# A graph layer on one core: 84 and 88 single-row loads per block instead of 76 and 76, with seven counts per list

## The chip, the cores and the metric

The kernel runs on one core of one Trainium2 chip. The metric is the device time of one launch in microseconds (us), the median of three runs. Engines are named as in the profile: PE (TensorE, matmul), DVE (VectorE), ACT (ScalarE), POOL (GpSimd) and SP (SyncE). SP and ACT also issue ordinary DMAs from their instruction streams; POOL issues the indirect ones.

## The reference

A message-passing layer over 50,000 nodes of 128 features and 1,650,000 edges, sorted by destination. Each edge carries the source row through one of two matrices, chosen by its type; the messages are summed by destination, a self term and a ReLU follow, and the result is added to the input and normalised.

```python
# x (50000, 128) f32; src, dst, edge_type_2 (1650000,) int32, dst sorted
src, dst = (edge_index[0], edge_index[1])
Xs = X[src]
m_data = Xs @ W_data.T + b_data
m_ctrl = Xs @ W_control.T + b_control
msg = jnp.where((edge_types == 0)[:, None], m_data, m_ctrl)
agg = jax.ops.segment_sum(msg, dst, num_segments=X.shape[0])
out = agg + (X @ W_self.T + b_self)
return jax.nn.relu(out)
# outside: x = _layernorm(x + that, axis=-1)
```

## The kernel before, in words

**Blocks and steps.** The edge list is cut into `NBLK` blocks, here 430, each of two steps (`Q = 2`). In a step, most source rows are fetched by 14 (`R`) indirect gathers of 128 rows each, issued by POOL (L551): 28 gathers in a block. A list of `S = 76` further rows of the step is fetched one row at a time, each row of 512 bytes by a DMA of its own (`single_rows`, L568 to L593): the list of the first step by SP, that of the second by ACT. `F = 53` more edges per step are edges whose source the block's nodes provide, and are handled by DVE (`fill`). A block so covers `BE = 28 * 128 + 2 * (53 + 76) = 3842` edges. The first block and the last have gathers only; the last has what is left over, 17 gathers. Lists therefore exist for blocks 1 to 428.

**What a list issues.** The byte offsets of a list's rows lie in SBUF (`off_g`). `values_load_multi_w_load_instructions` (L580) loads up to `LOAD = 28` of them into the issuing engine's registers with one TENSOR_LOAD; then each row takes a register move and a DMA (L585). A list of 76 is so loaded in pieces of 28, 28 and 20. After every so many rows the engine raises the semaphore `issued[q]` by one (`mark`, L530): `R = 14` times in a list.

**What sets the order.** The schedule is written out by hand. In the turn of block `b`, the lists of block `b + FAR` (`FAR = 4`) are issued. Each list fills a buffer of its own, `y1` in the pool `one`; there are `ALONE = 10` of them, five per step, so a list's first row waits until PE has used the list five blocks earlier (matmul L613). On the other side, `pace` (L532) makes POOL wait before gather `k` of block `b`, from block 4 on, until step `k % 2`'s list of block `b + LAG` (`LAG = 1`) has been issued up to mark `k // Q`, that is `k // 2`. So POOL can't run further ahead than the lists of the next block.

**Other work on the same engines.** ACT, after every second list, computes the square root of the layernorm (`root`, ACTIVATE L677), and DVE's `store` (L683) waits for it. SP stores a block's output rows after its list (L691), loads a strip of `x` every eighth block (L490) and the edge tables every tenth (L196 to L200). DVE builds the one-hot matrices and their counts (L507, L515), and the filled-in indices (L395 to L416). PE multiplies one-hot by rows (L607) and by the single rows (L613).

Of the kernel before, what the change touches and what calls it, by code (L numbers as in the profile page):

```python
# [33 lines left out]
R = 14  # L34
W = 64
Q = 2
PASS = 7
B = 124
C = R * Q
F = 53  # L40
LATE = 10
FX = LATE + F
R1 = R + 1
# [2 lines left out]
SIZES = [P] * R  # L46
SIZE = sum(SIZES)
CE = Q * SIZE
S = 76
LOAD = 28  # L50
BE = CE + Q * (F + S)
NBLK = 2 + (E + LATE - CE) // BE
REST = E + LATE - CE - (NBLK - 2) * BE
REST_ROWS = [min(n, max(0, REST - q * SIZE - sum(SIZES[:r]))) for q in range(Q) for r, n in enumerate(SIZES)]
# [9 lines left out]
LAG = 1  # L64
# [18 lines left out]
TBL = GROUPS * GB  # L83
# [8 lines left out]
def plain(b):  # L92

    return b == 0 or b >= NBLK - 1
# [6 lines left out]
def straight(ctx, tc, c, x, x_t, edges_t, edges_f, edges_1, dst_first, first_p, out):  # L101
# [13 lines left out]
    nc = tc.nc  # L115
# [73 lines left out]
    def offsets(g):  # L189
        off = eds.tile([GB * Q, S], I32, name="off")  # L190
        nc.vector.tensor_scalar(off, one_g.pop(g), float(ROW), float((N - 1) * ROW), op0=ALU.mult, op1=ALU.min)
        off_g[g] = off

    def load_edges(g):
# [3 lines left out]
        nc.sync.dma_start(f.rearrange("b m f -> b (m f)"), edges_f[g * GB:(g + 1) * GB, :])  # L198
        one = eds.tile([GB * Q, S], I32, name="sd1", bufs=1)
        nc.sync.dma_start(one, edges_1[g * GB * Q:(g + 1) * GB * Q, :])  # L200
# [249 lines left out]
    def chunks_of(b, q):  # L450

        n = RCH if b == NBLK - 1 else C if b < NBLK else 0
        return range(q * R, max(q * R, min((q + 1) * R, n)))

    def column(k):
        return k // R * R1 + k % R

    def steps_of(b):
        return [q for q in range(Q) if len(chunks_of(b, q))]
# [12 lines left out]
    ys, ohs, cnts, accs, xTs, pos, hs, mvs, sds, os_ = {}, {}, {}, {}, {}, {}, {}, {}, {}, {}  # L472
# [54 lines left out]
    issued_no, asked, marks = [0] * Q, [0] * Q, {}  # L527

    def mark(q):
        (nc.scalar if q else nc.sync).sem_inc(issued[q], 1)  # L530
        issued_no[q] += 1

    def pace(b, k):

        if b < FAR:
            return
        q = k % Q
        if (b + LAG, q) in marks:
            n = marks[b + LAG, q] + k // Q
            if n > asked[q]:  # L540
                nc.gpsimd.wait_ge(issued[q], n)
                asked[q] = n

    def gathers(b, ks):
        i = pass_no[0] % SLOTS
        pass_no[0] += 1
        y = gat.tile([P, R, D], F32, name="y")
        for k in ks:
            pace(b, k)
            r = REST_ROWS[k] if b == NBLK - 1 else SIZES[k % R]  # L550
            copy = nc.gpsimd.indirect_dma_start(  # L551
                out=y[:r, k % R, :].bitcast(U8), out_offset=None, in_=x_rows,
                in_offset=bass.IndirectOffsetOnAxis(ap=idxs[b][:r, column(k):column(k) + 1], axis=0))
            copy.then_inc(landed[i], 16)
            tc.no_tile_sem_insts.add(copy.ins.name)
            tc.add_to_no_dep_group(f"rows{b}_{ks[0]}", copy.ins)
        seen[i] += 16 * len(ks)
        wait = nc.tensor.wait_ge(landed[i], seen[i])  # L558
        tc.declare_fence(wait.ins, group=f"rows{b}_{ks[0]}")
        return y  # L560
# [3 lines left out]
    got = [0] * ALONE  # L564
# [3 lines left out]
    def single_rows(b):  # L568
        if plain(b):
            return  # L570
        g, i = divmod(b, GB)
        for q in range(Q):
            j = alone_no[0] % ALONE
            alone_no[0] += 1
            marks[b, q] = issued_no[q]
            y = one.tile([S, D], F32, name="y1")
            for s0 in range(0, S, LOAD):
                n = min(LOAD, S - s0)
                at = i * Q + q
                _, regs = nc.values_load_multi_w_load_instructions(  # L580
                    off_g[g][at:at + 1, s0:s0 + n], engines=[ACT if q else SP], min_val=0, max_val=(N - 1) * ROW,
                    skip_runtime_bounds_check_because=CLAMPED)
                for k, r in enumerate(regs):
                    r = nc.s_assert_within(r, 0, (N - 1) * ROW, skip_runtime_bounds_check_because=CLAMPED)
                    copy = (nc.scalar if q else nc.sync).dma_start(y[s0 + k:s0 + k + 1, :].bitcast(U8),  # L585
                                               x_bytes[bass.ds(r, ROW)].rearrange("(p e) -> p e", e=ROW))
                    copy.then_inc(alone[j], 16)
                    tc.no_tile_sem_insts.add(copy.ins.name)
                    tc.add_to_no_dep_group(f"single{b}_{q}", copy.ins)
                    while issued_no[q] - marks[b, q] < (s0 + k + 1) * R // S:  # L590
                        mark(q)
            got[j] += 16 * S
            singles[b, q] = y, alone[j], got[j]  # L593

    def products(b, q, ks):
        of_step = chunks_of(b, q)
        if b == NBLK - 1:
            ys[b, q] = gathers(b, ks)
        elif ks[0] == of_step[0]:
            ys[b, q] = gathers(b, of_step)  # L600
        y = ys[b, q]
        if ks[0] == 0:
            accs[b] = ps.tile([P, Q, 3, W], F32, name="acc")
        acc = accs[b][:, q]
        for k in ks:
            r = REST_ROWS[k] if b == NBLK - 1 else SIZES[k % R]
            nc.tensor.matmul(acc[:, :2, :].rearrange("p t w -> p (t w)"), y[:r, k % R, :], ohs[b][:r, column(k), :],  # L607
                             start=k == of_step[0], stop=k == of_step[-1] and plain(b))
        if ks[-1] == of_step[-1] and not plain(b):
            y, landed_1, n = singles.pop((b, q))  # L610
            wait = nc.tensor.wait_ge(landed_1, n)
            tc.declare_fence(wait.ins, group=f"single{b}_{q}")
            nc.tensor.matmul(acc[:, :2, :].rearrange("p t w -> p (t w)"), y, ohs[b][:S, q * R1 + R, :], start=False, stop=True)  # L613
        if ks[-1] == of_step[-1] and q == steps_of(b)[-1]:
            for t in range(2):
                nc.tensor.matmul(accs[b][:, :q + 1, 2, :], to_row[:, t, :], cnts[b][:, :q + 1, t * W:(t + 1) * W],  # L616
                                 start=t == 0, stop=t == 1)
# [107 lines left out]

    columns(0)
    single_rows(1)
    spread(1)
    fill(1)
# [13 lines left out]
    for b in range(2, FAR):  # L743
        single_rows(b)
    made, fresh = 2, [2]
    ready = []
    for b in range(NBLK):
# [23 lines left out]
        if b == NBLK - 1:  # L771
            layer(b - 1)
            moments(b - 1)
            root(pair(b - 1))
            own_part(b)
            store(pair(b - 1))
            for done in pair(b - 1):
                store_rows(done)
            for step, ks in passes_of(b):
                if ks:  # L780
                    products(b, step, ks)
            break
# [3 lines left out]
        if b + FAR < NBLK:  # L786
            single_rows(b + FAR)
        for q, (step, ks) in enumerate(passes_of(b)):
            if ks:
                products(b, step, ks)  # L790
# [28 lines left out]
    b = NBLK - 1  # L819
# [340 lines left out]
```

## Time and profile before

| what | value |
|---|---|
| median of 3 runs | 15066.82 us (15066.48 to 15069.68) |
| the profiled execution, its own time | 15065.38 us |
| its span, first to last instruction | 15063.7 us |
| granted TensorE clock, mean | 0.671 |
| HBM read, written | 870.39 MB, 27.30 MB |
| DMAs issued by SP and by ACT for single rows | 32528 each |
| indirect gathers by POOL | 12012 and 17 in the last block |

How to read it: the span is that of the one profiled execution, and durations below are from it; its own time is 1.7 us above its span, and the median 3.1 us above. The busy times count an engine's work, not the issue of DMAs, register moves or semaphores: SP has no busy time at all, and ACT almost none, though both issue rows most of the time. Their instruction streams show as SPq and ACTq in the timeline.

### The profile page before, as it was taken

The page shows a single profiled execution, that of the slowest core. Times are in us where ns is not written, and L with a number is a line of the kernel's source. Part 1 is how long each engine was busy: PE and PEld are TensorE (multiplying, and loading weights), DVE is VectorE, ACT ScalarE, POOL GpSimd, SP SyncE. Part 2 cuts the span into 40 slices and gives each one's busy share as a digit, 9 for nine tenths or more (in the row PEclk, how much of TensorE's full clock was granted, in tenths as well). Part 3 has the DMA queues.
Part 4 walks back from the last instruction along what each step waited for, and adds up shares of the span by engine and source line. Part 5 has one row for each costly group of instructions (what it writes and reads, how often), then busy time and mean ns, then how long its engine had stood idle before and what let it go on. Part 6 is the DMA issues. An engine that isn't in the chain of part 4 may idle for free. (4 is left out here: it accounts for less than half of the span.)

```text
span 15063.7 us, 244090 instructions
## 1 busy us (share of the span) xinstructions
PE 5857.4 (39%) x32862; PEld 5479.9 (36%) x32863; DVE 12073.6 (80%) x11957; ACT 67.2 (0%) x222; POOL 11376.7 (76%) x12039
## 2 busy tenths in 40 slices
PE   3433333333333333333333333333333333333333
PEld 3333333333333333333333333333333333333333
DVE  9878888877877788888888887878788888887875
ACT  0000000000000000000000000000000000000000
POOL 7777777777777777777777777777777777777777
PEclk7666666666666666666666666666666666666666
DMA  2222222222222222222222222222222222222222
GB/s 64 60 62 60 61 61 60 62 60 61 62 60 60 62 60 60 62 60 60 61 60 60 63 60 60 61 60 62 60 60 62 60 60 61 60 61 62 60 59 57
DMA packets 588595, 914.45 MB, mean 61 GB/s; under 512 B 262747, under 2 KB 381952, under 8 KB 586944
## 3 DMA queue, kind: packets, MB, share of 16 engines
q0 software_dynamic: 384928, 789.04, 20.8%
q1 hardware_dynamic: 136522, 92.72, 2.4%
q10 hardware_dynamic: 65494, 16.98, 0.6%
q14 instruction: 1384, 11.34, 0.2%
q8 instruction: 267, 4.37, 0.1%
HBM read 870.39 MB, written 27.30 MB: 60 GB/s over the span
## 5 line engine op out<-in xcount | busy, mean ns | idle before, releaser
L551 POOL DMA_INDIRECT y<-in_x,idx x12012 | 11359.3, 946 | 3667.3 <-issue 3075.1
L607 PE MATMUL acc<-oh,y 128*128 128x128 f32 x24058 | 4774.6, 384 | 8916.1 <-PEq L558 8871.1
L607 PEld LDWEIGHTS acc<-oh,y 128*128 128x128 f32 x24058 | 4571.4, 293 | 9247.8 <-issue 5053.0
L515 DVE TENSOR_REDUCE cnt<-oh 128x256 bf16<-128x3840 f32 x430 | 2834.7, 6592 | 14.7
L507 DVE TENSOR_TENSOR oh<-col,small 128x3840 f32<-128x3840 f32 x430 | 1781.5, 4143 | 0.0
L416 DVE TENSOR_REDUCE by<-new 128x126 bf16<-128x1890 f32 x428 | 1497.0, 3498 | 14.6
L621 DVE TENSOR_TENSOR sums<-acc,sums 128x192 f32 x860 | 307.3, 357 | 1341.1 <-PE acc L616 1292.9
L395 DVE COPY small<-cb 128x30 f32<-128x30 f32 x428 | 82.0, 192 | 1219.7 <-PE small L423 1219.7
L400 DVE TENSOR_TENSOR new<-m,small 128x1890 f32<-128x1890 f32 x428 | 909.0, 2124 | 14.7
L397 DVE TENSOR_TENSOR m<-rk,small 128x1890 f32<-128x1890 f32 x428 | 908.9, 2124 | 14.6
L404 DVE TENSOR_REDUCE v_new<-new 128x30 f32<-128x1890 f32 x428 | 907.9, 2121 | 14.7
L413 DVE TENSOR_TENSOR new<-m,small 128x1890 f32<-128x1890 f32 x428 | 905.8, 2116 | 0.0
L613 PE MATMUL acc<-oh,y 76*128 76x128 f32 x1712 | 334.0, 276 | 0.0
L651 PE MATMUL po<-wmsgT,sums 128*124 128x128 f32 x1720 | 304.5, 300 | 0.0
L613 PEld LDWEIGHTS acc<-oh,y 76*128 76x128 f32 x1712 | 265.6, 195 | 0.0
L641 PE MATMUL po<-own_w,xT 128*124 128x256 f32 x860 | 262.3, 386 | 0.8 <-DVE h L657 0.8
L637 DVE TENSOR_TENSOR sums<-pl,sums 128x372 f32<-128x372 f32 x428 | 233.2, 545 | 14.9
L651 PEld LDWEIGHTS po<-wmsgT,sums 128*124 128x124 f32 x1720 | 221.5, 188 | 53.0 <-issue 1.6
L448 DVE TENSOR_TENSOR pl<-pl,xT 128x248 f32<-128x248 f32 x428 | 181.7, 425 | 46.6 <-DVE xT L501 2.7
L649 PE MATMUL po<-bias,sums 3*124 3x128 f32 x860 | 208.3, 322 | 1.2 <-DVE sums L621 1.2
L649 PEld LDWEIGHTS po<-bias,sums 3*124 3x124 f32 x860 | 125.2, 183 | 149.3 <-issue 147.4
L501 DVE COPY xT<-xw 128x124 f32 x430 | 111.7, 260 | 77.4 <-issue 74.2
(147 smaller groups left out, 2915.1 us busy)
## 6 DMA issues: line engine op xcount, KB each, us to landing
y<-in_x SPq DMA_DIRECT2D x32528, 0.5 KB
y<-in_x ACTq DMA_DIRECT2D x32528, 0.5 KB
y<-in_x,idx POOLq DMA_INDIRECT x12012
xw<-in_x_t SPq DMA_DIRECT2D x54, 496.0 KB
out<-o SPq DMA_DIRECT2D x430, 62.0 KB
sdt<-in_edges_t SPq DMA_DIRECT2D x43, 450.0 KB
sdt_f<-in_edges_f SPq DMA_DIRECT2D x43, 14.8 KB
sd<-in_edges SPq DMA_DIRECT2D x43, 5.9 KB
```

The costliest lines, as they stand in the source:

```text
L397: nc.vector.tensor_tensor(m, rk_g[g][:, i, :, None].to_broadcast([P, C1, FX]), rank_no_ps[:, None, :].to_broadcast([P, C1, FX]), op=ALU.is ...
L400: nc.vector.tensor_tensor(new.rearrange("p (q r) f -> p q r f", r=R1), m.rearrange("p (q r) f -> p q r f", r=R1), vf.rearrange("p (q f) -> ...
L404: nc.vector.tensor_reduce(v, new, AX.X, ALU.add)
L413: nc.vector.tensor_tensor(old, m, cb[:, :, None].to_broadcast([P, C1, FX]), op=ALU.mult)
L416: nc.vector.tensor_reduce(by, old.rearrange("p (q r) f -> p q f r", r=R1), AX.X, ALU.add)
L507: nc.vector.tensor_tensor(oh, col_g[g][:, i, :, None].to_broadcast([P, C1, 2 * W]), num_ps[:, None, :].to_broadcast([P, C1, 2 * W]), op=AL ...
L515: nc.vector.tensor_reduce(cnt, ohs[b].rearrange("p (q r) w -> p q w r", r=R1), AX.X, ALU.add)
L551: copy = nc.gpsimd.indirect_dma_start(out=y[:r, k % R, :].bitcast(U8), out_offset=None, in_=x_rows, in_offset=bass.IndirectOffsetOnAxis(ap ...
L607: nc.tensor.matmul(acc[:, :2, :].rearrange("p t w -> p (t w)"), y[:r, k % R, :], ohs[b][:r, column(k), :], start=k == of_step[0], stop=k = ...
L613: nc.tensor.matmul(acc[:, :2, :].rearrange("p t w -> p (t w)"), y, ohs[b][:S, q * R1 + R, :], start=False, stop=True)
L649: nc.tensor.matmul(po, a[0:3, 2, :B], bias, start=False, stop=False)
L651: nc.tensor.matmul(po, a[:, t, :B], c["wmsgT"][:, t * D:(t + 1) * D], start=False, stop=t == 1)
```

## The change

The list of a block's first step (SP) grows from 76 rows to 84, loaded in three pieces of 28; that of the second step (ACT) from 76 to 88, loaded in pieces of 32, 32 and 24. Each list raises its semaphore 7 times instead of 14, and POOL's wait before gather `k` asks for mark `k * 7 // 28`. A block covers `3584 + 106 + 172 = 3862` edges, so the edges fit into 428 blocks instead of 430, with 10 gathers in the last. Buffers of the lists have 88 rows. The arrays on the host are laid out to match.

```diff
-S = 76
-LOAD = 28
-BE = CE + Q * (F + S)
+SINGLE = (84, 88)
+LOADS = (28, 32)
+S = max(SINGLE)
+MARKS = 7
+BE = CE + Q * F + sum(SINGLE)
...
-            n = marks[b + LAG, q] + k // Q
+            n = marks[b + LAG, q] + k * MARKS // C
...
-            for s0 in range(0, S, LOAD):
-                n = min(LOAD, S - s0)
+            for s0 in range(0, SINGLE[q], LOADS[q]):
+                n = min(LOADS[q], SINGLE[q] - s0)
...
-                    while issued_no[q] - marks[b, q] < (s0 + k + 1) * R // S:
+                    while issued_no[q] - marks[b, q] < (s0 + k + 1) * MARKS // SINGLE[q]:
                         mark(q)
-            got[j] += 16 * S
+            got[j] += 16 * SINGLE[q]
...
-            nc.tensor.matmul(acc[:, :2, :].rearrange("p t w -> p (t w)"), y, ohs[b][:S, q * R1 + R, :], start=False, stop=True)
+            nc.tensor.matmul(acc[:, :2, :].rearrange("p t w -> p (t w)"), y[:SINGLE[q], :], ohs[b][:SINGLE[q], q * R1 + R, :], start=False, stop=True)
```

In ACT's stream, one square root and the list behind it, before the change (`off` holds the offsets, `y_5307` is the list's buffer; a row "x27" stands for 27 DMAs of a row each; moves and marks are not shown):

```order
L677 ACTIVATE sd<-mv,eps 124x2 [waits DVE_49]
L580 TENSOR_LOAD off
L585 DMA y_5307<-in_x 1x512 [waits PE_sequencer_49,PE_49]
L585 DMA y_5307<-in_x 1x512 x27
L580 TENSOR_LOAD off
L585 DMA y_5307<-in_x 1x512 x28
L580 TENSOR_LOAD off
L585 DMA y_5307<-in_x 1x512 x20
```

The same place with the change:

```order
L679 ACTIVATE sd<-mv,eps 124x2 [waits DVE_49]
L582 TENSOR_LOAD off
L587 DMA y_5678<-in_x 1x512 [waits PE_sequencer_49,PE_49]
L587 DMA y_5678<-in_x 1x512 x31
L582 TENSOR_LOAD off
L587 DMA y_5678<-in_x 1x512 x32
L582 TENSOR_LOAD off
L587 DMA y_5678<-in_x 1x512 x24
```

Nothing changes its place; the three pieces grow from 28, 28 and 20 rows to 32, 32 and 24.

In POOL's stream, the first gathers of block 4, where the waits for the marks begin (`issued0` is SP's semaphore, `issued1` ACT's), before the change:

```order
L551 DMA y<-in_x,idx 128x512 [waits DVE_49,PE_sequencer_49,issued0,PE_49]
L551 DMA y<-in_x,idx 128x512 [waits issued1]
L551 DMA y<-in_x,idx 128x512 [waits issued0]
L551 DMA y<-in_x,idx 128x512 [waits issued1]
L551 DMA y<-in_x,idx 128x512 [waits issued0]
```

The same place with the change:

```order
L553 DMA y<-in_x,idx 128x512 [waits DVE_49,PE_sequencer_49,issued0,PE_49]
L553 DMA y<-in_x,idx 128x512 [waits issued1]
L553 DMA y<-in_x,idx 128x512 x2
L553 DMA y<-in_x,idx 128x512 [waits issued0]
L553 DMA y<-in_x,idx 128x512 [waits issued1]
```

Before, every gather waits for a mark, SP's and ACT's in turn; now two in four do, for marks that stand for 12 rows of SP or 12 to 13 of ACT instead of 5 to 6.

More of the change, by code (lines that the diff above doesn't have):

```diff
@@ L1122 @@
         rest = a[CE:].reshape(TBL - 1, BE)
-        steps = rest.reshape(TBL - 1, Q, SIZE + S + F)
+        step_at = [sum(SIZE + s + F for s in SINGLE[:q]) for q in range(Q)]
         cols = np.full((TBL, Q, R1, P), pad, np.int32)
@@ L1127 @@
             cols[0, :, r, :n] = a[:CE].reshape(Q, SIZE)[:, at:at + n]
-            cols[1:, :, r, :n] = steps[:, :, at:at + n]
+            for q in range(Q):
+                cols[1:, q, r, :n] = rest[:, step_at[q] + at:][:, :n]
             cols[NBLK - 1, :, r, :n] = rest[NBLK - 2, :CE].reshape(Q, SIZE)[:, at:at + n]
-        cols[1:NBLK - 1, :, R, :S] = steps[:NBLK - 2, :, SIZE:SIZE + S]
+        for q, n in enumerate(SINGLE):
+            cols[1:NBLK - 1, q, R, :n] = rest[:NBLK - 2, step_at[q] + SIZE:][:, :n]
         if k == "src":
@@ L1133 @@
         fills = np.full((TBL * Q, FX), pad, np.int32)
-        own = steps[:NBLK - 2, :, SIZE + S:].reshape((NBLK - 2) * Q, F)
+        own = np.stack([rest[:NBLK - 2, step_at[q] + SIZE + n:][:, :F] for q, n in enumerate(SINGLE)], 1).reshape(-1, F)
         fills[Q:(NBLK - 1) * Q, LATE:] = own
```

## The prediction

> **What bounds the kernel now.** I read the page's busy times first, then POOL's groups and timeline, then the streams of SP and ACT, which the busy times leave out.
>
> ```profile
> PE 5857.4 (39%) x32862; PEld 5479.9 (36%) x32863; DVE 12073.6 (80%) x11957; ACT 67.2 (0%) x222; POOL 11376.7 (76%) x12039
> L551 POOL DMA_INDIRECT y<-in_x,idx x12012 | 11359.3, 946 | 3667.3 <-issue 3075.1 <-ACTq L530 254.6 <-SPq L530 228.4
> L551 POOL DMA_INDIRECT y<-in_x,sdt x17 | 16.0, 939 | 5.2 <-issue 4.0 <-PE acc L607 0.6 <-PE po L651 0.3
> 3.19 1.13 POOL L551 DMA_INDIRECT y<-in_x,idx  x1 [1.07 <-DMA idx<-in_edges_t]
> ...
> 7007.59 0.94 POOL L551 DMA_INDIRECT y<-in_x,idx  x1 [0.30 <-issue]
> 7008.84 0.94 POOL L551 DMA_INDIRECT y<-in_x,idx  x1 [0.30 <-issue]
> 7010.08 0.95 POOL L551 DMA_INDIRECT y<-in_x,idx  x1 [0.30 <-ACTq L530]
> ...
> 15048.96 0.88 POOL L551 DMA_INDIRECT y<-in_x,sdt  x1 [0.30 <-issue]
> ```
>
> No engine is over 80% busy, but POOL never stops. A gather takes 946 ns and is followed by 0.30 us, whether the profile names "issue" or a mark of ACT (L530) as the releaser: a gap that is the same with and without a wait is the cost of the next instruction, no wait. From the first gather at 3.19 to the last at 15048.96 there are 12028 intervals, 15045.77 / 12028 = 1.251 us each. A block of 28 gathers is 35.03 us, and 12029 gathers are the whole time but 3.2 us ahead and 15063.7 - 15048.96 - 0.88 = 13.9 us behind. DVE (12073.6 / 430 = 28.1 us a block) and PE have room.
>
> SP and ACT must issue one list each in these 35.03 us. How much of it they need shows in ACT's timeline at two places (start, length, rows issued in a run). Early, after an even start, and late:
>
> ```profile
> 15.34 94.72 ACTq L585 DMA_DIRECT2D y<-in_x  x226
> ...
> 808.40 65.19 ACTq L585 DMA_DIRECT2D y<-in_x  x152
> 873.76 0.29 ACT L677 ACTIVATE sd<-mv,eps 124x2 f32<-124x2 f32 x1 [67.18 <-issue]
> 875.88 64.12 ACTq L585 DMA_DIRECT2D y<-in_x  x152
> ...
> 1276.91 64.41 ACTq L585 DMA_DIRECT2D y<-in_x  x152
> 1341.50 0.29 ACT L677 ACTIVATE sd<-mv,eps 124x2 f32<-124x2 f32 x1 [66.44 <-DVE idx L408]
> 1343.89 36.29 ACTq L585 DMA_DIRECT2D y<-in_x  x83
> ```
>
> ```profile
> 7052.58 29.66 ACTq L585 DMA_DIRECT2D y<-in_x  x76
> 7086.98 29.68 ACTq L585 DMA_DIRECT2D y<-in_x  x76
> 7116.83 0.30 ACT L677 ACTIVATE sd<-mv,eps 124x2 f32<-124x2 f32 x1 [69.81 <-DVE at L430]
> 7123.15 6.77 ACTq L585 DMA_DIRECT2D y<-in_x  x19
> ```
>
> Early, ACT works without a pause: between the end of a list at 808.40 + 65.19 = 873.59 and the next one's first row at 875.88 lie 2.29 us, square root and register load included. From 808.40 to 1343.89 it issues 16 lists, **33.47 us a list**. It is faster than POOL, gets ahead, and then runs into its buffers: late, 7082.24 to 7086.98 are 4.74 us, of which 4.74 - 2.29 = 2.45 is a wait, and a list without it would be 29.66 + 2.29 = **31.95 us**. So ACT has between 1.6 and 3.1 us of a block to spare. SP has as little, by its timeline and, in the last row, its waits (us in total, times, longest):
>
> ```profile
> 806.46 30.89 SPq L585 DMA_DIRECT2D y<-in_x  x76
> 837.59 0.28 SPq L691 DMA_DIRECT2D out<-o  x1
> 840.03 30.85 SPq L585 DMA_DIRECT2D y<-in_x  x76
> 871.11 0.28 SPq L691 DMA_DIRECT2D out<-o  x1
> 873.63 30.75 SPq L585 DMA_DIRECT2D y<-in_x  x76
> SPq L585 <- PE acc L613: 803.6, 340, 4.0
> ```
>
> At full rate a list with its output store takes 840.03 - 806.46 = 33.57 us; over the whole span it waits 803.6 us for buffers, 803.6 / 428 = 1.9 us a list.
>
> **The change part by part.** *POOL.* Two blocks of 28 gathers go, and 17 gathers in the last become 10: 56 + 7 = 63 gathers fewer, 63 x 1.251 = **78.8 us** off, if POOL stays the bound. The span would be 11966 x 1.251 + 3.2 + 13.9 = 14986.6 us. The cover of POOL's pace is that both lists of the next block are issued in time; POOL waits for their marks.
>
> *ACT.* The price of a row, of a mark and of a register comes from these rows: four rows without a mark, two with one between them, and the loads of 28 registers and of 20.
>
> ```profile
> 7080.73 1.18 ACTq L585 DMA_DIRECT2D y<-in_x  x4
> 7080.35 0.62 ACTq L585 DMA_DIRECT2D y<-in_x  x2
> L585 ACTq DMA_DIRECT2D y<-in_x x32528: 227/228/617, 15.3 to 14891.8; - x200
> L580 ACTq TENSOR_LOAD <-off x1: 1947/1947/1947, 7062.0 to 7062.0; - x1
> L580 ACTq TENSOR_LOAD <-off x1: 1548/1548/1548, 7073.8 to 7073.8; - x1
> ```
>
> An issue itself lasts 0.228 us (min, median and max of all issues in the third row), so a row comes every (1.18 - 0.228) / 3 = 0.317 us, and with a mark after 0.62 - 0.228 = 0.39, so a mark is 0.07. Eight registers more make a load 0.40 us longer, 0.05 each. A list gains 12 rows, 12 x 0.317 = 3.80 us, and 12 registers, 0.60, and loses 7 marks, 0.49: **+3.9 us**. There are still three loads and half a square root in a list, and no DMA of another kind is on ACT. At full rate a list would take 31.95 + 3.9 = 35.9 us by the late rows, and 33.47 + 3.9 = 37.4 by the early ones; with the early rows' wider spacing (33.47 against 31.95, or 5%) on the new rows as well, 37.6. All three are over 35.03, so ACT has no pause left, and the 78.8 us saved on POOL are not seen.
>
> *SP.* Eight rows more, 2.54 us, eight registers, 0.40, seven marks fewer, 0.49 less: +2.45, and 33.57 + 2.45 = 36.0 us. That is over POOL too, but under what I take for ACT, so it is hidden there. What SP issues beside its list (stores, strips, edge tables) stays as it was.
>
> *POOL's waits.* It now asks for a mark before two gathers in four. The last mark asked in a block is the sixth of the seven, ACT's row 76 of 88, close to the end of the list, as before (mark 13 of 14). Coarser marks bunch POOL's waits but don't change how many rows must be out at a block's end, so I price them at nothing in either direction: the gather's gap is 0.30 us beside a mark or not.
>
> *Behind ACT.* The square root for a pair of blocks stands behind the list, and DVE's `store` waits for it; a late list holds DVE. DVE needs 28.1 us of a block that will last 36 or more, and builds indices five blocks ahead, so it catches up inside the pair. PE's matmul over 84 or 88 rows instead of 76 adds no instruction.
>
> **How the time follows.** ACT's first row starts at 15.3 us and it then issues 426 lists (blocks 1 to 426) without a pause, p us each; POOL is released for the end of block 425 with the last of them, and then has 28 + 10 gathers without marks left, 38 x 1.251 = 47.5, and 13.9 us of tail. With the 2.3 us that don't follow the last list: span = 15.3 + 426 p - 2.3 + 47.5 + 13.9 = 426 p + 74.4. The ends of p are 35.9 and 37.6. The kernel will be nearer the early rows, where ACT has no pause and issues at once with SP almost always; but SP, at 36.0, will wait for buffers about a microsecond a list, as it does late, so I take **p = 36.9**. That gives a span of 15793.8; the median of the runs shown lies 3.1 us over the profiled span, so **15797 us**, 4.8% over 15066.82. The ends give 15371 and 16095.
>
> **The rivals.** *POOL stays the bound*, 14986.6 + 3.1 = 14990 us, 0.5% faster. Its place is ACT's list and its price the 12 rows; it holds if a longer list fits into 35.03 us. From the most favourable 31.95 us only 3.08 may be added, and with 0.60 - 0.49 for registers and marks the 12 rows would have to come at (3.08 - 0.11) / 12 = 0.248 us each. The issue alone lasts 0.228, and no row shows a spacing under 0.317. For it speaks only that the late waits are the longer part of the trace. The Trainium skill, DMA: Bandwidth & Descriptors, section Issuing engines are not separate DMA queues, says that issuing from several engines saves only the sequencer's time for starting a DMA, which is usually small against the DMA; by that rule the added rows would cost next to nothing, and the time would be this rival's. Here the trace disagrees: the 0.317 us are what fills ACT's stream.
>
> *ACT is over POOL, but only just.* If the list runs as late and registers cost nothing, p is 31.95 + 3.80 - 0.49 = 35.3 and the time 426 x 35.3 + 74.4 + 3.1 = 15115 us, 0.3% slower. That needs SP under 35.3 as well, which its early 33.57 + 2.45 speaks against.
>
> *One row at a time for both streams.* If the 0.228 us of an issue keep the other stream out, 172 rows need 39.2 us a block, 426 x 39.2 + 77.5 = 16777 us. Early, 152 rows would need 34.66 but took 33.47, so the issues overlap somewhat; against this rival also stands that rows are mostly evenly spaced. The Trainium skill, Perfetto Trace Analysis, section on DMA instructions by HWDGE, says that the generator of descriptors is locked for one sequencer while it is used, and that a wait for the lock is part of the profiled time. By it the sum would move towards this rival; the 33.47 us show that at most a part of the 0.228 can be locked.
>
> **Chances.** ACT bound with p from 35.9 to 37.6: 0.88. POOL stays the bound: 0.04. Just over: 0.04, of which 0.01 within 0.2%. One row at a time or a further loss: 0.04. The range 15450 to 16100 leaves out the lowest fifth of a microsecond of p, which SP's own 36.0 makes unlikely, and the rivals, some 0.15 in all. A measurement of this kernel can tell about 0.2% from no change. Faster 0.04, same 0.01, slower 0.95.
>
> **What would show it.** In the changed profile ACT's timeline should have runs of 88 rows with about 2.5 us between them and no longer pause, a list every 36 to 37.6 us from the first to the last; POOL should wait visibly longer than 0.30 us on ACT's marks (L532) in every block, its busy share falling to some 72%; SP should still wait on PE for its buffers, about a microsecond a list; DVE should wait for the square root before L685. If POOL's gaps stay at 0.30 us, the ACT term is wrong. If ACT's list is shorter than 35.9 us, the price of a row, a register or a pause is; if POOL waits mainly on SP, the order of the two lists is.

## The result, and the profile after

The changed kernel takes **16111.9 us** (median of four runs, 16111.58 to 16114.0) against 15066.65 us before, 1.0694 times as long (95% interval 1.0676 to 1.0713). The profiled execution has a span of 16110.1 us.

The page of the changed kernel: busy times, and the groups of POOL's gathers and of DVE's wait for the square root (busy time and mean, then the idle time ahead of them and who ended it).

```profile
PE 6097.5 (38%) x32698; PEld 5539.4 (34%) x32699; DVE 12027.6 (75%) x11909; ACT 66.7 (0%) x221; POOL 11313.9 (70%) x11976
L553 POOL DMA_INDIRECT y<-in_x,idx x11956 | 11302.7, 945 | 4777.0 <-issue 3227.2
L685 DVE RECIPROCAL rstd<-sd 124x2 f32<-124x2 f32 x215 | 35.6, 166 | 3674.9 <-ACT sd L679 3674.9
```

Its waits (in total, times, longest), POOL's and then SP's:

```profile
POOL y L553 <- ACTq L532: 1421.6, 1127, 2.9
POOL y L553 <- SPq L532: 53.1, 170, 1.5
...
SPq L587 <- PE acc L615: 423.8, 165, 3.6
SPq L587 <- PEq L613: 140.3, 49, 5.0
```

A gather takes 945 ns as before, and there are fewer of them, but POOL now waits for ACT's marks: 1421.6 us in 1127 waits, of which 0.30 us each is the old gap, so some 1080 us are real. They are nearly all of the 1123 us by which the span, 16110.1 us, exceeds the 14986.6 us that POOL would have needed alone. They are not long, 2.9 us at most; POOL's timeline shows one:

```profile
7047.97 0.95 POOL L553 DMA_INDIRECT y<-in_x,idx  x1 [0.30 <-issue]
7050.95 0.94 POOL L553 DMA_INDIRECT y<-in_x,idx  x1 [2.03 <-ACTq L532]
7052.20 0.95 POOL L553 DMA_INDIRECT y<-in_x,idx  x1 [0.31 <-PE acc L609]
```

ACT's own timeline has no pause any more, early or late, and ends with the last list:

```profile
843.61 74.10 ACTq L587 DMA_DIRECT2D y<-in_x  x176
917.89 0.29 ACT L679 ACTIVATE sd<-mv,eps 124x2 f32<-124x2 f32 x1 [76.33 <-issue]
920.23 73.32 ACTq L587 DMA_DIRECT2D y<-in_x  x176
...
1073.96 24.29 ACTq L587 DMA_DIRECT2D y<-in_x  x64
...
7034.52 72.86 ACTq L587 DMA_DIRECT2D y<-in_x  x176
7107.57 0.29 ACT L679 ACTIVATE sd<-mv,eps 124x2 f32<-124x2 f32 x1 [75.09 <-issue]
7109.95 70.03 ACTq L587 DMA_DIRECT2D y<-in_x  x168
...
15977.03 69.64 ACTq L587 DMA_DIRECT2D y<-in_x  x176
```

From 843.61 to 1073.96 it issues six lists, 38.4 us each; from 7034.52 to 7109.95 two, 37.7 each. In between lies the point where SP, which needs less, runs into its buffers and begins to wait (564 us in all, 1.3 a list). Over the whole run a list takes (16110.1 - 74.4) / 426 = **37.64 us**, by the prediction's sum. That is where the time came from: a block is no longer as long as 28 gathers but as long as ACT's list.

One more thing changed. The windows view (mean share of the DMA engines' time that is busy, and GB/s, at the end of a row) from 4000 to 8000 us, before and after:

```profile
4000.00:8000.00 4000.00, 1559.38 (x8748) 1461.80 (x8748) 3205.76 (x3171) 16.84 (x57) 3023.74 (x3200) 0.67 0.23 61
```

```profile
4000.00:8000.00 4000.00, 1532.35 (x8133) 1391.87 (x8133) 2986.36 (x2935) 15.64 (x53) 2816.05 (x2980) 0.63 0.27 57
```

The DMA engines are busier (0.27 against 0.23) while they move less. The kernel before shows the same where both streams run without a pause: from 800 to 1344 us its share is 0.28, at the same 61 GB/s as later. So there were two questions: is it ACT's list that sets the pace, and why is the list 37.64 us and not the 36.9 of the forecast.

### The profile page after: what moved, and what is told of

Read it like the earlier page. It is cut to its first block, busy times and chain, and to the rows that moved or that the text cites. A ratio compares the mean times of both kernels' runs of the same rounds, so it can differ in the third digit from the quotient of the medians.

```text
span 16110.1 us, 253999 instructions
## 1 busy us (share of the span) xinstructions
PE 6097.5 (38%) x32698; PEld 5539.4 (34%) x32699; DVE 12027.6 (75%) x11909; ACT 66.7 (0%) x221; POOL 11313.9 (70%) x11976
## 5 line engine op out<-in xcount | busy, mean ns | idle before, releaser
L609 PEld LDWEIGHTS acc<-oh,y 128*128 128x128 f32 x23932 | 4466.1, 289 | 10137.5 <-issue 8047.2
L685 DVE RECIPROCAL rstd<-sd 124x2 f32<-124x2 f32 x215 | 35.6, 166 | 3674.9 <-ACT sd L679 3674.9
L425 PE MATMUL small<-ones_b,by 128*126 128x1 bf16 x426 | 73.0, 172 | 2696.2 <-DVE oh L509 2696.2
L388 PE MATMUL small<-v_f,row_of 74*128 74x126 bf16 x426 | 104.8, 247 | 2393.1 <-DVE at L432 2366.0
L615 PE MATMUL acc<-oh,y 84*128 84x128 f32 (+1 forms) x1704 | 396.4, 321 | 0.0
L643 PE MATMUL po<-own_w,xT 128*124 128x256 f32 x856 | 350.6, 502 | 0.8 <-DVE h L659 0.8
L653 PE MATMUL po<-wmsgT,sums 128*124 128x128 f32 x1712 | 345.4, 331 | 0.0
L615 PEld LDWEIGHTS acc<-oh,y 84*128 84x128 f32 (+1 forms) x1704 | 329.0, 240 | 0.0
L653 PEld LDWEIGHTS po<-wmsgT,sums 128*124 128x124 f32 x1712 | 253.9, 213 | 62.3 <-issue 22.7
```

Source lines behind the costliest of these rows:

```text
L653: nc.tensor.matmul(po, a[:, t, :B], c["wmsgT"][:, t * D:(t + 1) * D], start=False, stop=t == 1)
```

## The experiments

Theory A is the prediction's: each stream needs the sum of its own instructions, and the longer one sets the pace. Theory B is that the streams of SP and ACT share something behind them, so that the rows of both together count. The kernels are the changed one with other numbers; the short names are those of the runs.

**Each stream alone, and fewer rows beside ACT's 88.**

```diff
-SINGLE = (84, 88)
+SINGLE = (84, 76)    # a1, LOADS (28, 28)
+SINGLE = (76, 88)    # a2
+SINGLE = (28, 88)    # a3
```

> Lists of 84 rows (SP) and 76 (ACT), 7 marks each, 429 blocks. Theory (a stream that needs more than POOL's 35.03 us for its list sets the pace, whichever of the two): SP at full rate took 36.6 us a list of 84 in the changed kernel's early part, so about 36.3 here, 427 x 36.3 + 77 = 15580 us, POOL waiting on SP's marks, ACT pausing 2 us or more a list. Rival (only ACT's longer list costs, SP's fits): POOL stays the bound with 12004 gathers, 12004 x 1.251 + 20 = 15037 us.

> Lists of 76 rows (SP) and 88 (ACT), 7 marks each, 429 blocks. Theory (ACT's list alone sets the pace, and its rows come slower the more SP issues beside them): 37.0 to 37.4 us a list, 427 x 37.2 + 77 = 15960 us, SP pausing about 4 us a list. Rival (SP's issues don't touch ACT's): 37.6 us a list as in the changed kernel, 427 x 37.6 + 77 = 16130 us.

> SP's list cut to 28 rows, ACT's left at 88, 434 blocks. Theory (what the list takes over the sum of its parts, 37.6 against 35.9, is lost to SP issuing at the same time): ACT's list falls to 35.8 to 36.2 us, 432 x 36.0 + 77 = 15630 us, and nearly all rows stand 0.318 us apart. Rival (the rows are slowed by something else, POOL's gathers or the fetching of instructions): 37.4 us or more, 432 x 37.5 + 77 = 16280 us.

a1 took 15232.93 us, 1.0106 (1.0077 to 1.0136) of the 15075 us before. In its timeline SP has no pause, and a list takes 34.8 to 35.1 us:

```profile
7011.53 31.95 SPq L587 DMA_DIRECT2D y<-in_x  x84
7043.70 0.28 SPq L693 DMA_DIRECT2D out<-o  x1
7046.36 32.31 SPq L587 DMA_DIRECT2D y<-in_x  x84
7078.89 0.28 SPq L693 DMA_DIRECT2D out<-o  x1
7081.47 32.46 SPq L587 DMA_DIRECT2D y<-in_x  x84
```

With strips and edge tables it is (15230.8 - 74.4) / 427 = 35.5 us on average. So SP's part of the change costs time by itself, against the rival; but less than the theory's 36.3, which was read where ACT's list of 88 stood beside it.

a3 took 15792.66 us. ACT's list is (15791.0 - 74.4) / 432 = 36.4 us:

```profile
7067.78 69.89 ACTq L587 DMA_DIRECT2D y<-in_x  x176
7137.84 0.30 ACT L679 ACTIVATE sd<-mv,eps 124x2 f32<-124x2 f32 x1 [72.11 <-issue]
7140.29 59.80 ACTq L587 DMA_DIRECT2D y<-in_x  x150
```

The stream of ACT is the same as in the changed kernel, and SP issues 28 rows beside it instead of 84: 1.2 of the 37.64 us go. That is just over the theory's 35.8 to 36.2 and far from the rival's 37.4. I take the rest of ACT's list, 36.4, as its own; it is still 0.5 over the lowest sum of the forecast.

a2's launch took 36.8 ms, since with these lists the kernel's test of its own assumptions (the branch behind `found`) sent it through the general path after the blocks; only the first part of its trace is used. There ACT's list with 76 rows on SP is (7113.06 - 7040.09) / 2 = 36.5 us, hardly more than with 28 (ACT's timeline, and behind the dots SP's):

```profile
7040.09 70.45 ACTq L587 DMA_DIRECT2D y<-in_x  x176
7110.72 0.29 ACT L679 ACTIVATE sd<-mv,eps 124x2 f32<-124x2 f32 x1 [72.69 <-issue]
7113.06 70.03 ACTq L587 DMA_DIRECT2D y<-in_x  x176
...
7038.64 0.28 SPq L693 DMA_DIRECT2D out<-o  x1
7047.80 28.95 SPq L587 DMA_DIRECT2D y<-in_x  x76
7076.99 0.28 SPq L693 DMA_DIRECT2D out<-o  x1
```

The theory's 37.0 to 37.4 fails here: the loss doesn't grow evenly with SP's rows. It comes when SP is nearly always issuing; here it pauses, 9.2 us between 7038.64 and 7047.80 in this list. The rival's 37.6 fails too.

**The marks.**

```diff
-MARKS = 7
+MARKS = 14                # a4, lists of 84 and 88
```

```diff
-SINGLE = (84, 88)
+SINGLE = (76, 76)         # b3, MARKS 7, LOADS (28, 28)
```

> The changed kernel with 14 marks a list instead of 7, so that POOL's waits are as fine as before. Theory (a mark costs ACT 0.07 us and coarse marks cost POOL nothing): 426 x 7 x 0.07 = 209 us more, 16320 us. Rival (waiting on coarse marks is what slows POOL): faster than the changed kernel's 16112 us.

> The kernel before with 7 marks a list instead of 14, the lists at 76 rows each: the part of the change that is only marks. All theories: POOL is the bound with 12029 gathers, 15067 us, no difference; ACT and SP pause 0.5 us longer a list. If POOL waited on the coarser marks, it would be slower by what its gaps on L532 are over 0.30 us.

a4 took 16128.85 us, 17 more than the changed kernel, where theory A asked for 209, and not less, as coarse marks would have it. b3 took 15067.71 us, 1.000 (0.9991 to 1.001): the marks alone change nothing. Its early stretch, where both streams run without a pause, is the more telling:

```profile
805.59 64.00 ACTq L587 DMA_DIRECT2D y<-in_x  x152
...
1341.64 18.20 ACTq L587 DMA_DIRECT2D y<-in_x  x44
```

16 lists in 536.05 us are 33.50 us each, with 7 marks; before, with 14 marks, the same stretch had 33.47. At full rate a mark of ACT's stream costs nothing, as if the stream had slack. The lengths of the single issues in the traces show where the slack is: over these 16 lists ACT's issues last 0.263 us on average with 7 marks and 0.256 with 14. By 76 rows that is 0.5 us, as much as 7 marks of 0.07.

**As many rows in all, spread evenly.**

```diff
-SINGLE = (84, 88)
+SINGLE = (80, 80)         # b1, LOADS (28, 28)
+SINGLE = (78, 78)         # b2, LOADS (28, 28)
+SINGLE = (79, 79)         # b4, LOADS (28, 28)
```

> Lists of 80 and 80 rows, 7 marks each, 429 blocks: as many rows in a block as with 84 and 76, but neither stream near 35.03 us by its own sum (SP 35.3 - 4 x 0.375 = 33.8, ACT 36.4 - 8 x 0.375 = 33.4). Theory A (each stream's own list is the bound): POOL stays the bound, 12004 gathers, 12004 x 1.251 + 20 = 15037 us. Theory B (something that both streams share, such as the DMA engines behind them, takes so many rows of both in a time: 172 rows in 37.6 us, 160 in 35.4): 35.4 us a block again, 427 x 35.4 + 77 = 15190 us or a little more, both streams without a pause.

> Lists of 78 and 78 rows, 7 marks each, 430 blocks, 12015 gathers. Theory A: POOL is the bound, 12015 x 1.251 + 20 = 15051 us, 0.1% faster than before. Theory B: 156 rows in 156 / 160 x 35.4 = 34.5 us, under POOL's 35.03, so the same 15051 us.

b1 took 15148.4 us (15115.7 to 15159.62), 1.0056 (1.0041 to 1.0072) of before: theory A's 15037 fails, theory B's 15190 is near. Neither stream pauses, and ACT's 80 rows take 35.2 us:

```profile
7045.31 67.90 ACTq L587 DMA_DIRECT2D y<-in_x  x160
7113.39 0.29 ACT L679 ACTIVATE sd<-mv,eps 124x2 f32<-124x2 f32 x1 [69.89 <-issue]
7115.78 4.24 ACTq L587 DMA_DIRECT2D y<-in_x  x11
```

Where both streams run at full rate, then, 152 rows take 33.47 us and 160 take 35.24, **0.220 us for each row of either stream**. The changed kernel's early rows are of the same kind; there SP issues 14 lists between these two rows:

```profile
806.27 34.13 SPq L587 DMA_DIRECT2D y<-in_x  x84
...
1317.61 26.48 SPq L587 DMA_DIRECT2D y<-in_x  x64
```

That is 36.5 us a list of SP's beside 38.4 of ACT's, 84 / 36.5 + 88 / 38.4 = 4.59 rows in a microsecond, 0.218 us each. By 0.220 the 164 rows of a2 would need 36.1 us, less than the 36.4 that ACT's list takes in a3; so SP's 76 rows could add little there.

b2 took 15054.5 us, 0.9991 (0.9982 to 1.0000) of before, where both theories had 15051: POOL is the bound again, with 14 gathers fewer. The difference is at the edge of what can be told from no change.

> Lists of 79 and 79 rows, 7 marks each, 429 blocks, 12011 gathers: the longest even pair whose 158 rows x 0.220 us = 34.8 us stay under POOL's 35.03. Theory C: POOL stays the bound, 12011 x 1.251 + 20 = 15046 us, 0.15% faster than before and 0.06% faster than with 78 and 78. Theory A (each stream by its own sum) gives the same time but long pauses of both streams, 1 to 2 us a list; theory C a pause of 0.2 us.

b4 went through the general path like a2 (43.3 ms), and on a chip on which the kernel before took 19.48 ms instead of 15.07. Nothing is read from it.

**What the rows share: the gathers.** In c1 a gather has 64 rows, so that half of the gathered rows is missing from the sum; in e1 only 2 of 14 gathers of a step are issued, in f1 7 of 14.

```diff
-            r = REST_ROWS[k] if b == NBLK - 1 else SIZES[k % R]
+            r = min(64, REST_ROWS[k] if b == NBLK - 1 else SIZES[k % R])   # c1, gathers and matmuls
...
-        for k in ks:
+        for k in [k for k in ks if k % R < 2]:      # e1 (f1: < 7), gathers and matmuls
```

> The changed kernel (84 and 88 rows) with each gather cut to 64 rows of 128, and the matmuls over those 64 alone: half of the gathered rows is left out of the sum. Nothing in SP's and ACT's streams changes. Theory B with the DMA engines as what is shared: gathers take half their time there, so ACT falls to what it needs with SP nearly idle, 36.4 us a list, 426 x 36.4 + 77 = 15580 us. Rival (SP and ACT slow each other where they issue, whatever the DMA engines do): 37.5 us a list, 16060 us or more.

c1 took 15957.45 us; ACT's list is (7176.04 - 7026.85) / 4 = 37.3 us (the last row is ACT's issues over the run: shortest, median and longest in ns):

```profile
7026.85 72.13 ACTq L587 DMA_DIRECT2D y<-in_x  x176
...
7101.51 72.01 ACTq L587 DMA_DIRECT2D y<-in_x  x176
...
7176.04 23.95 ACTq L587 DMA_DIRECT2D y<-in_x  x63
...
L587 ACTq DMA_DIRECT2D y<-in_x x37488: 234/235/675, 15.7 to 15891.6; - x200
```

Half of the gathered bytes bring back 0.3 of 1.2 us: by the time alone that is nearer the rival, which had SP and ACT slow each other alone. But the last row shows something that need not come from the gathers: not one of ACT's issues is under 0.234 us, where in the changed kernel the shortest lasts 0.227 and the median 0.228. The two runs of e1 below, of one kernel, differ in the same way. 88 rows by 0.007 us are 0.6 us a list. Without them c1's list would be an estimated 36.7 us, and half-size gathers would bring back 0.9 of the 1.2. SP's issues don't have this (227 and 228 ns in both runs), and SP's lists between 800 and 1344 us go the same way: 36.5 us in the changed kernel, 35.6 in c1, 35.2 in e1. By this estimate c1 speaks against the rival too, and so does e1:

> The changed kernel (84 and 88 rows) with 2 of each step's 14 gathers and their matmuls; the other 12 are left out of the sum. SP's and ACT's streams are as they were, POOL has almost nothing to do. If the gathers take part in what slows the rows: ACT falls to what it needs with SP nearly idle, 36.4 us a list, about 15540 us. If SP and ACT slow each other alone: 37.2 us a list, as with half gathers, about 15880 us.

> Two of each step's 14 gathers, the others left out of the sum, beside the changed kernel on the same chip. If the gathers take part in what slows the rows: 36.4 us a list, 15578 us as in the call before. If SP and ACT slow each other alone: 37.2 us or more.

e1 took 15579.5 us on one chip and 15789.35 on another. The timeline of the second, where both streams are at full rate, ACT's rows and then SP's, and last ACT's issues in the first run and in the second:

```profile
1050.69 71.20 ACTq L590 DMA_DIRECT2D y<-in_x  x176
...
1198.23 1.76 ACTq L590 DMA_DIRECT2D y<-in_x  x5
...
1068.65 32.18 SPq L590 DMA_DIRECT2D y<-in_x  x84
1101.05 0.28 SPq L696 DMA_DIRECT2D out<-o  x1
1103.53 16.54 SPq L590 DMA_DIRECT2D y<-in_x  x43
...
L590 ACTq DMA_DIRECT2D y<-in_x x37488: 12/228/604, 15.5 to 15534.2; - x200
...
L590 ACTq DMA_DIRECT2D y<-in_x x37488: 3/235/588, 15.6 to 15743.8; - x200
```

SP's list takes 34.9 us and ACT's 147.54 / 4 = 36.9, both at once: 84 / 34.9 + 88 / 36.9 = 4.79 rows in a microsecond, where all gathers left 4.5 to 4.6. The 36.9 is the median issue of 0.235 us again; in the first run, at 0.228, ACT's list is (15577.8 - 74.4) / 426 = 36.4 us, as in a3, where SP had 28 rows. So with few gathers the two streams hardly slow each other, and with few rows on SP (a3) the gathers hardly slow ACT: it takes SP, ACT and the gathers together, as far as chips of two kinds can be set side by side.

These runs have a flaw. Both runs of e1, and those of d1, f0 and f1, were on chips on which the kernel before takes 19.46 to 19.48 ms (below, chips of the first kind are those with 15.07). The second e1, f1 and the last d1 stand beside f0, the changed kernel on the same chip, and are compared with it only; the first e1 has no such run beside it, and neither e1 nor f1 was run on a chip of the first kind.

> The changed kernel as it is, on the chip on which the three others of this call run: 16112 us and 37.6 us a list if the chip gives the kernel before its 15067 us, and the measure for the three others if not.

> The changed kernel with 7 of each step's 14 gathers, of 128 rows each, and their matmuls; the other 7 are left out of the sum. As many gathered bytes as with 14 gathers of 64 rows, half as many gathers. If what slows the rows goes by the number of gathers' DMAs: between the 37.2 us a list of half-size gathers and 36.4, about 36.6, 15670 us. If it goes by their rows or bytes: 37.2 us as there, about 15920 us.

> The changed kernel with 256 bytes of each single row, half of the single rows' features left out, beside the changed kernel on the same chip. Theory C (the shared cost goes by the number of rows): as the changed kernel, 37.5 us a list, 16100 us. Theory D (it goes by bytes): 36.4 us a list, 15580 us.

f0 took 21037.31 us, 1.08 times the 19456.57 of the kernel before on that chip: slower by about as much as on the other chips (1.07), but by SP's list, as POOL's waits in its trace show (us in total, times, longest):

```profile
POOL y L553 <- SPq L532: 4740.5, 1270, 6.5
POOL y L553 <- ACTq L532: 72.0, 137, 1.3
```

f1, with half of the gathers, took 15793.27 us, e1 15789.35. That the two agree is chance: in f1 POOL waits for SP (2190.0 us, against 40.3 for ACT), so SP's list sets the time, (15791.6 - 74.4) / 426 = 36.9 us, while in e1 it is ACT's. Against f0 SP's list falls from 49.2 to 36.9 us with half the gathers, so on these chips too the rows' slowness hangs on the gathers. f1's question, whether it goes by the number of gathers or by their bytes, was put for ACT's list and isn't answered. d1, single rows of 256 bytes instead of 512 (half of their features left out), took 20995.54, 21043.15 and 20920.46 us on three chips. The last stands beside f0's 21037.31, 0.6% less, but d1's own three times lie as far apart; so no share that goes by the rows' bytes is shown there, and on a chip of the first kind it was not measured.

**Where the 1.2 us sit.** The traces have the length of every issue. ACT's last 0.253 us on average in the changed kernel, 0.240 in a2 and 0.238 in a3. Between the changed kernel and a3 that is 88 x 0.0148 = 1.3 us a list, all of the loss: the rest of a list, 15.4 us, is the same in both, and the issues themselves stretch. The packets of ACT's rows stretch as well. By its counts queue q10 is ACT's, with two packets a row and 438 others in each run; before, changed kernel, a3 (packets, MB, share of 16 engines' span):

```profile
q10 hardware_dynamic: 65494, 16.98, 0.6%
...
q10 hardware_dynamic: 75414, 19.54, 1.4%
...
q10 hardware_dynamic: 76470, 19.81, 0.6%
```

By these shares a packet took about 22, 48 and 20 ns. Whether the slower packets hold up the issues, or only go with them, is not shown.

## Why the prediction was right, and where it wasn't

**Direction and the stream that sets the pace: right.** ACT lost its pause, POOL's 63 fewer gathers (11956 and 10 remain) are not seen, and the time is the number of lists by ACT's list. The sum's form holds within 2 us: ACT's 426 lists run from 15.7 to 15977.03 + 69.64 = 16046.67 us, which is 37.64 us each without using the sum, and 63.4 us come behind them where it had 47.5 + 13.9 = 61.4. ACT's next list begins 920.23 - 843.61 - 74.10 = 2.5 us after the last one, as forecast, POOL waits on ACT's marks (70% busy, 72 forecast), SP waits for PE 1.3 us a list (about one forecast), and DVE waits 3674.9 us for the square root and is hidden behind ACT.

**The size of p: wrong.** The step that failed is the one for ACT's list ("so I take **p = 36.9**"), a term of 36.9 us with ends at 35.9 and 37.6 that measured 37.64. 0.74 us by 426 lists are the 315 us between 15797 and 16112, and the upper end of the range, 16100, lay 12 us under the time. It was summed from row, register and mark prices on top of a list of before, the late one at the lower end and the early one at the upper. a3 shows the part that I take as ACT's own, 36.4: the sum from the late lists was 0.5 short. 0.3 of that is the two lists that were read, which took 29.66 us from first row to last where the lists from 4000 to 8000 us average 29.95; the rest was not traced. The other 1.2 us come only with SP's 84 rows beside it (37.64 against 36.4 with 28 rows and 36.5 with 76), and, by c1 and e1, with the gathers. The sum had this in it only as the 1.5 us by which the early lists were longer than the late ones, and took about half of that.

The reading behind it was that an issue lasts 0.228 us, "min, median and max". The row says 227/228/617: the median is 0.228, but the longest issue is 0.617, and a tenth of ACT's issues were over 0.25 us before, 23% in the changed kernel. The prices of 0.317 us a row and 0.07 us a mark were taken from six rows that had none of these, and so left out what stretches.

**The marks: mispriced.** 7 marks were to give back 0.49 us. At full rate they give back nothing (33.50 against 33.47 us with half the marks; 17 us instead of 209 with twice as many), since the issues take up the time that marks leave.

**The third rival had the right form.** It let SP's and ACT's rows exclude each other for the whole 0.228 us of an issue and gave 39.2 us a list. Read as a rate, the early lists of before (152 rows in 33.47 us, 0.220 each) give 172 x 0.220 = 37.9 us for a list of the changed kernel: measured 38.4 early, and 37.6 to 37.7 later, where SP waits. I had the number and used it to dismiss the rival instead of as the price. As a lock between the two streams the rival is wrong, though. In the changed kernel's trace 59% of ACT's issues begin while one of SP's is running, and they last no longer than the others (0.253 against 0.252 us on average); and e1's 4.79 rows in a microsecond by 0.228 us would be 1.09 of the time. The Trainium skill, Perfetto Trace Analysis, section on DMA instructions by HWDGE, has the descriptor generator locked for one sequencer while it is used; e1 leaves room for a locked part of at most 1 / 4.79 = 0.21 us of the 0.228.

**The rival that POOL stays the bound** fell: 12 rows more on ACT and 8 on SP were not free. The rule beside it, that starting a DMA usually takes little beside the DMA itself (the Trainium skill, DMA: Bandwidth & Descriptors, Issuing engines are not separate DMA queues), doesn't help for 512-byte rows issued one by one: here the issues fill the streams. a1 and b1 are the narrow cases, 1.1% and 0.6% slower; at 156 rows (b2) POOL is the bound.

**Open.** What SP, ACT and the gathers share isn't settled. Half the gathered bytes with as many gathers gives back 0.3 to 0.9 of the 1.2 us, depending on whether the 0.007 us of an issue are counted; a seventh of the gathers gives back all of it in the first e1, on a chip of the other kind. On the first kind of chip the number of gathers, their bytes and the rows' bytes were not told apart. Why ACT's median issue is 0.228 us in some executions and 0.235 in others is open too.

## What to carry to other kernels

When a stream that issues DMAs is filled up, price it from a stretch in which all streams run without a pause, and as a rate of what they issue together as well as by the sum of its own instructions; the longer of the two holds (a2 and a3 went by ACT's own 36.4 us, b1 and the changed kernel by the rate). Read the longest of a group beside its median. A pause of 2.45 us a block is not 2.45 us of free capacity if a second stream wants the same; here the most that was seen to fit was 156 rows a block (b2), and 160 did not (b1). Work that is taken off a bound engine and given to one that is "0% busy" must be checked in that engine's instruction stream, since the busy times leave issue out.

## What the runs showed of the hardware

Two streams of single-row DMAs beside full gathers issue 4.5 to 4.6 rows in a microsecond together (152 in 33.47 us, 160 in 35.24; 84 / 36.5 + 88 / 38.4), and 4.79 beside few gathers on a chip of the other kind. What changes is the length of an issue: 0.253 us on average in ACT's stream, 0.238 when SP has 28 rows. When the streams are saturated, small instructions between the rows (marks of 0.07 us) cost nothing (33.50 and 33.47 us with 7 and 14).

The chips differ. On three of the five chips of the experiments the kernel before took 19.46 to 19.48 ms, against 15.07 on the others. In f0's trace there SP's list is the longer one, and a single issue of SP's lasts up to 1.45 us, where the changed kernel has 0.60 at most on a chip of the first kind. With half of the gathers or fewer the changed kernel takes 15.6 to 15.8 ms there. Why was not tried.
